# Gathered rows in eleven buffers, and a wait on TensorE in every third batch of gathers

## The chip, the cores and the metric

One core of a Trainium2 chip runs the kernel. The time is the device time of one launch in microseconds, the median of several runs on the same chip.

## The reference

One layer of a graph network on 12,500 nodes with 160 values each (64 scalars and 32 vectors of three) and 400,000 edges, which are sorted by their target node:

```python
h = jnp.maximum(_layernorm(x, axis=-1), 0.0)
x0 = h[:, :64]; x1 = h[:, 64:].reshape(n, 32, 3)
y0 = x0 @ W_l1_0 * a / 8                       # a: one value per node
y1 = einsum('nuc,uv->nvc', x1, W_l1_1) * a / sqrt(32)
w  = silu(edge_attr_16 @ fc_W1 / 4) @ fc_W2 / 8   # 192 weights per edge: w_a, w_b, w_c, w_d
ys0 = y0[src]; ys1 = y1[src]                   # a row of y for each edge
e0 = edge_attr_4[:, :1]; e1 = edge_attr_4[:, 1:]
mid_a = w_a * ys0 * e0
mid_d = w_d * einsum('euc,ec->eu', ys1, e1) / sqrt(3)
mid_b = (w_b * ys0)[:, :, None] * e1[:, None, :]
mid_c = (w_c * e0)[:, :, None] * ys1
z0 = zeros.at[dst].add(concat(mid_a, mid_d)); z1 = zeros.at[dst].add(concat(mid_b, mid_c))
out = x + self-connection of h + z0, z1 mapped by W_l2_0, W_l2_1
```

## The kernel before

**Stages.** First the nodes: layer norm, relu and the two maps, 8 tiles of 128 nodes at a time. The rows of y go to a table `y_d` in HBM, the self-connection into `acc`, which stays in SBUF. Then the edges in 3125 tiles of 128. Four tiles (`GT`) are a batch, 782 batches in all, and three batches (`K = TG // GT`) share one selection matrix of 12 tiles. Sums over edges of one target are matmuls with that selection matrix, gathered in PSUM over groups of 24 tiles (the first three fifths of the edges) or 12.

**One step of the edge loop.** Iteration `b` of the loop in the last part of the function does, in program order:

- `load_xe`: asks on SP's queue for the block of edge features that batch `b + AHEAD` needs.
- `weigh(b + 2)` (L609, L611): four matmuls on TensorE give the edge weights of a batch in PSUM (`pw`, two of them in turn), and then ACT puts three edge values of each edge beside them.
- `lift_rows(b + 2)` (L520): ACT multiplies the gathered rows by an edge value, into `yge`.
- `dots_of(b + 1)` (L525, L527) and `products(b + 1)` (L531, L532, L535, L536) on DVE; each third batch also `select` (L628).
- `load(b + AHEAD)` (L571 to L584, the gathers in L579): four indirect DMAs issued by POOL, each of 128 rows of `y_d` by the source numbers in `src_sb`, into one of `YB` buffers `yg`. A buffer is free again when DVE's L531 and ACT's L520 of its batch have read it.
- `sums(b)` (L648) on TensorE, and what belongs to a finished group (`turn`, `map_sums`, `accumulate`); each second batch `hidden` (L592, L597), the first layer of the edge network.

**Queues.** TensorE, ACT and DVE run in exactly this order, since the loop stands in a manual schedule. POOL and SP do not: their instructions are ordered by the tile framework, which puts a gather on POOL's queue when the things it waits for come, by its own reckoning. A POOL instruction that waits holds up all behind it.

**The wait by hand.** `load` gives the first gather of a batch (`k == 0`) one more thing to wait for: the last weight matmul of batch `b - AHEAD + 2`, whose name `weigh` has kept in `weighed`. With `YB = 9` and `AHEAD = YB + 1 = 10` that is eight batches back. The buffer itself came from the batch nine back.

**Made batches.** For 24 batches (48, 72, ... 432 and 498, 540, ... 750; all multiples of three) y is not gathered. The rows of x for them were gathered while the nodes were worked on (L375, into `xr`, a pool `nrx` of 12 buffers, then to `xr_d` in HBM), and TensorE, DVE and ACT make y from them in the gaps of the edge loop (`made_load` to `made_leave`). For such a batch `load` returns before the gathers and the wait.

**Ahead of the loop** nine batches are loaded (`min(YB, NB)`), then `load(YB)` for the tenth.

Of the kernel before, what the change touches and what calls it, by code (L numbers as in the profile page):

```python
# [29 lines left out]
SP = 256 - WN // 4  # L30
TG = 12
EG = 8
YB = 9
WIDE = 3, 5
GN = 8
HN = 2
# [9 lines left out]
def kernel(  # L46
# [31 lines left out]
    NB = (T + GT - 1) // GT  # L78
# [32 lines left out]
    def made(b):  # L111

        return made_at.index(b) if b in made_at else None
# [30 lines left out]

    ygp = ctx.enter_context(tc.tile_pool(name="yg", bufs=YB))

# [50 lines left out]
    def relate_edges(q, evp, lim):  # L197

        lo, hi = q * EG * TG, min((q + 1) * EG * TG, T)
        over = evp.tile([P, EG * TG], F32, name="over")  # L200
        up = evp.tile([P, EG * TG], F32, name="up")
        for g, k, t, n in runs_of(lo, hi):
            v = drel[:, t:t + k * n].rearrange("p (s t) -> p s t", t=n)
            o = over[:, t - lo:t - lo + k * n].rearrange("p (s t) -> p s t", t=n)
            nc.vector.tensor_tensor(o, v, lim[:, g:g + k].unsqueeze(2).to_broadcast([P, k, n]), ALU.is_ge)
            nc.vector.tensor_tensor(v, v, nbase[:, g:g + k].unsqueeze(2).to_broadcast([P, k, n]), ALU.add)
        nc.vector.tensor_reduce(fars[:, q:q + 1], over[:, :hi - lo], AX.X, ALU.max)

        nc.vector.tensor_scalar(up[:, :hi - lo], drel[:, lo:hi], float(WN), -float(WN), ALU.is_ge, ALU.mult)
        nc.vector.tensor_add(drel[:, lo:hi], drel[:, lo:hi], up[:, :hi - lo])  # L210

        nc.vector.scalar_tensor_tensor(drel[:, lo:hi], over[:, :hi - lo], float(2 * ZR), drel[:, lo:hi],
                                       op0=ALU.mult, op1=ALU.add)

    def any_far(cnt):

        nc.vector.tensor_reduce(far, fars, AX.X, ALU.max)
        nc.tensor.matmul(cnt, far, one, start=True, stop=True)
        nc.vector.tensor_scalar(far_i, cnt, 1.0, None, ALU.min)
# [67 lines left out]
    def load_xe(blk):  # L287

        if blk not in blocks:
            xe = ld.tile([P, 512], F32, name="xe")  # L290
            v = e16[blk * P:(blk + 1) * P, :].rearrange("(s k f) (h c) -> k s (f h) c", s=4, k=2, h=2)
            for k in range(2):
                nc.sync.dma_start(xe[:, 256 * k:256 * (k + 1)], v[k])
            blocks[blk] = xe

    def e4_load(q):

        if q * EG < NU and q not in raws:
            lo, hi = q * EG * TG, min((q + 1) * EG * TG, TP)
            raw = ld.tile([P, EG * TG, 4], F32, name="raw")  # L300
            nc.sync.dma_start(raw[:, :hi - lo, :].rearrange("p t c -> p (t c)"), e4[:, lo * 4:hi * 4])
            raws[q] = raw
# [26 lines left out]
    engines = {mybir.EngineType.PE, mybir.EngineType.Activation, mybir.EngineType.DVE}  # L329
    with (  # L330
        tc.tile_pool(name="nr", bufs=1) as nrp,
        tc.tile_pool(name="nrx", bufs=12) as nrx,
        tc.tile_pool(name="ny", bufs=2) as ny,
        tc.tile_pool(name="ns", bufs=3) as ns,
        tc.tile_pool(name="nh", bufs=4) as nh,
# [204 lines left out]
    with (  # L540
# [9 lines left out]
        leaving, weighed = [], {}  # L550
# [5 lines left out]
        def next_px():  # L556
            turns["px"] += 1
            return pxs[turns["px"] % 2]

        K = TG // GT  # L560
        AHEAD = YB + 1

        short = NB - 2 if NB > 1 and (NB - 1) * GT % TG else NB

# [3 lines left out]
        def tiles_of(b):  # L568
            return list(range(first_of(b), first_of(b + 1)))

        def load(b):  # L571
            r = made(b)
            if r is not None:
                rows[b] = xms[r]
                return
            yg = ygp.tile([P, GT, D], F32, name="yg")
            rows[b] = yg
            for k, t in enumerate(tiles_of(b)):
                ins = nc.gpsimd.indirect_dma_start(  # L579
                    out=yg[:, k, :], out_offset=None, in_=y_d,  # L580
                    in_offset=bass.IndirectOffsetOnAxis(ap=src_sb[:, t:t + 1], axis=0))
                if k == 0 and b - AHEAD + 2 in weighed:
                    tc.add_manual_dep(ins.ins, weighed[b - AHEAD + 2], mybir.DependencyInfo(
                        mybir.DependencyClass.Sync, mybir.DependencyReason.DATA), reason="no further ahead of the weights")  # L584

        def hidden(s):

            if 2 * s < NB:
                xe = blocks[s * 2 * GT // BT]
                r = slice(32 * (s % 4), 32 * (s % 4 + 1))  # L590
                ph = next_px()
                nc.tensor.matmul(ph, w1[r, :], xe[r, :], start=True, stop=True)  # L592
                leaving.append(lambda: activate(s, ph))
# [20 lines left out]
        def lift_rows(b):  # L614
            lifted[b] = part.tile([P, GT, D], F32, name="yge")
            lift(lifted[b], rows[b], e4_of(b), len(tiles_of(b)))
# [15 lines left out]
        def dots_of(b):  # L632
            tmp = part.tile([P, GT, 3, M1], F32, name="tmp")
            dot(tmp, wts[b], rows[b], len(tiles_of(b)))

        def products(b):
            pr = prod.tile([P, GT, PC], F32, name="pr")
            multiply(pr, wts.pop(b), rows.pop(b), lifted.pop(b), len(tiles_of(b)))
            prs[b] = pr
# [150 lines left out]
        def all_leave():  # L790
            todo = leaving[:]
            leaving.clear()
            for f in todo:
                f()

        order = tc.manual_schedule(engines={mybir.EngineType.PE, mybir.EngineType.Activation, mybir.EngineType.DVE})
        with order:
            e4_load(0)
            for blk in range(min(AHEAD - 1, NB - 1) * GT // BT + 1):
                load_xe(blk)  # L800
            for b in range(min(YB, NB)):
                load(b)
            relate_edges(0, part, lim)
            for s in range(3):
                hidden(s)
                all_leave()
            if NQ == 1:
                any_far(next_px()[0:1, 0:1])
            for pw in pws:
                nc.vector.tensor_copy(pw[:, :, SP:], iota[:, 0:WN].rearrange("p (k c) -> p k c", k=GT))  # L810
            for b in range(min(2, NB)):
                weigh(b)
                lift_rows(b)
            dots_of(0)
            if YB < NB:
                load(YB)
            select(0, wts[0])
            products(0)
            last_batch = [(t - 1) // GT for t in ends]
            turns_at, maps_at, adds_at = {}, {}, {}  # L820
            for g, e in enumerate(last_batch):
                at_end = e + 4 >= NB
                t = e + (1 if at_end else 2)
                m = t + (1 if at_end else 2 if (t + 2) % 2 else 3)
                turns_at.setdefault(t, []).append(g)
                maps_at.setdefault(m, []).append(g)
                a = m + (1 if at_end else 2)
                adds_at.setdefault(a + 1 if a == NB - 3 else a, []).append(g)
            for b in range(NB + 3):
                u, k = divmod(b, K)  # L830
                due(at_start, b)
                if b + AHEAD < NB:
                    load_xe((b + AHEAD) * GT // BT)
                if b < NB:
                    q, r = divmod(b, EG * K)
                    if r == 0:
                        e4_load(q + 1)
                    if r == EG * K - 8 and q + 1 < NQ:
                        relate_edges(q + 1, part, lim)
                    if r == EG * K - 4 and q + 2 == NQ:  # L840
                        any_far(next_px()[0:1, 0:1])
                if b + 2 < NB:
                    weigh(b + 2)
                all_leave()
                due(on_scalar, b)
                if b + 2 < NB:
                    lift_rows(b + 2)
                if b + 1 < NB:
                    dots_of(b + 1)
                    if k == K - 1:  # L850
                        select(u + 1, wts[b + 1])
                    products(b + 1)
                if b + AHEAD < NB:
                    load(b + AHEAD)
                for g in adds_at.get(b, []):
                    accumulate(g)
                    leave_before(g + 1)
                due(on_vector, b)
                if b < NB:
                    sums(b)  # L860
                for g in turns_at.get(b, []):
                    turn(g)
                for g in maps_at.get(b, []):
                    map_sums(g)
                if b % 2 == 0:
                    hidden((b + 6) // 2)
                due(on_tensor, b)
# [137 lines left out]
```

## Time and profile before

| | |
|---|---|
| median of 3 runs | 4818.65 us (4807.77 to 4824.67) |
| profiled execution | 4859.38 us, span 4857.6 us |
| mean granted TensorE clock | 0.905 |
| PE busy | 4063.7 us, 84% of the span |
| DVE busy | 3514.5 us, 72% |
| POOL busy | 2970.2 us, 61%, of which 2873.3 in 3029 gathers of L579 |
| ACT busy | 1762.0 us, 36% |
| DMA engines | 22.0% of 16 engines' span for the gathers' queue, 68 GB/s of HBM over the span |

Busy is the time in which an instruction of the engine runs. Behind the `<-` of a group stands what ended the idle time ahead of it: an engine with its tile and line, or `issue` where nothing that the profile shows was waited for. In the timeline a row gives the start, the duration, the engine and its line, and in brackets the idle time ahead of it.

### The profile page before, as it was taken

To read this page: it belongs to the slowest core of one execution; us is meant where nothing else is said; L and a number is where in the kernel's file an instruction comes from. 1 tells how busy PE (TensorE), PEld (TensorE's weight loads), DVE (VectorE), ACT (ScalarE), POOL (GpSimd) and SP (SyncE) were. 2 spreads that over 40 slices of the span, in tenths; PEclk is the share of its full clock that TensorE was granted. 3 is DMA by queue.
4 is the path that set the end of the run, shared out by engine and by line. 5 is a ranking of instruction groups with operands and counts; after the bars stand their busy time and mean duration, and the time that the engine had idled before them with its cause. 6 is when DMAs were issued, how large, how long until landed. Compare 5 with 4: busy or idle time off the path is not lost. (4 is left out here: it accounts for less than half of the span.)

```text
span 4857.6 us, 55990 instructions
## 1 busy us (share of the span) xinstructions
PE 4063.7 (84%) x16409; PEld 2349.2 (48%) x16409; DVE 3514.5 (72%) x6817; ACT 1762.0 (36%) x5610; POOL 2970.2 (61%) x3132
## 2 busy tenths in 40 slices
PE   5588888888888888888888888888888888888888
PEld 4344444444444444444444444454545455545554
DVE  4477777777777777777777776777777777777777
ACT  4333333333333333333333333333333333333333
POOL 6566566566666666666666666666666666666663
PEclk8788898999998889999999999899989999999899
DMA  7422222222222222222222222222222222232222
GB/s 212 122 60 60 63 65 62 64 61 62 63 66 64 62 65 61 62 63 66 65 62 66 62 64 61 63 63 64 66 58 66 61 65 61 65 104 61 62 61 59
DMA packets 228623, 335.20 MB, mean 69 GB/s; under 512 B 55099, under 2 KB 171911, under 8 KB 228055
## 3 DMA queue, kind: packets, MB, share of 16 engines
q0 software_dynamic: 150000, 256.20, 22.0%
q1 hardware_dynamic: 64642, 67.02, 4.5%
q10 hardware_dynamic: 13668, 8.36, 0.6%
q8 instruction: 130, 2.13, 0.2%
q14 instruction: 183, 1.49, 0.1%
HBM read 307.49 MB, written 23.88 MB: 68 GB/s over the span
## 5 line engine op out<-in xcount | busy, mean ns | idle before, releaser
L579 POOL DMA_INDIRECT yg<-y_d,src_sb x3029 | 2873.3, 949 | 1775.7 <-issue 827.8
L648 PE MATMUL pz<-pr,sel 128*128 128x384 f32 x6250 | 2515.7, 549 | 88.5 <-issue 59.9
L648 PEld LDWEIGHTS pz<-pr,sel 128*128 128x128 f32 x6250 | 1256.4, 211 | 1061.9 <-issue 508.9
L609 PE MATMUL pw<-w,hT 64*128 64x192 f32 x6250 | 833.3, 370 | 582.2 <-DVE pr L536 315.5
L611 ACT ACTIVATE pw<-raw 128x12 f32<-128x12 f32 (+1 forms) x782 | 140.2, 179 | 2973.4 <-remote 1215.2
L520 ACT ACTIVATE yge<-yg,raw 128x160 f32<-128x160 f32 x3029 | 1041.7, 421 | 0.0
L609 PEld LDWEIGHTS pw<-w,hT 64*128 64x128 f32 x6250 | 553.4, 197 | 974.9 <-issue 523.0
L525 DVE TENSOR_TENSOR tmp<-yg,pw 128x384 f32<-128x384 f32 (+1 forms) x758 | 416.0, 549 | 710.0 <-ACT pw L611 661.6
L532 DVE TENSOR_TENSOR pr<-pr,pw 128x768 f32<-128x768 f32 (+1 forms) x782 | 745.3, 953 | 27.0
L527 DVE TENSOR_REDUCE yg<-tmp 128x128 f32<-128x384 f32 (+1 forms) x758 | 450.0, 594 | 430.5 <-ACT yge L520 370.9
L628 DVE TENSOR_TENSOR sel<-pw,drel 128x1536 f32<-128x1536 f32 (+1 forms) x261 | 455.1, 1744 | 0.0
L592 PE MATMUL px<-xe,w 32*128 32x512 f32 x782 | 443.3, 649 | 13.5 <-issue 8.3
L531 DVE TENSOR_TENSOR pr<-pw,yg 128x384 f32<-128x384 f32 (+1 forms) x758 | 419.8, 554 | 17.8
L536 DVE TENSOR_TENSOR pr<-pw,yge 128x384 f32<-128x384 f32 (+1 forms) x782 | 427.9, 547 | 0.0
L535 DVE TENSOR_TENSOR pr<-pw,yge 128x256 f32<-128x256 f32 (+1 forms) x782 | 326.2, 417 | 0.0
L597 ACT ACTIVATE hT<-px 128x512 f32<-128x512 f32 x391 | 228.5, 585 | 11.3 <-PE px L592 10.5
L592 PEld LDWEIGHTS px<-xe,w 32*128 32x128 f32 x782 | 115.5, 185 | 214.1 <-issue 151.9
L675 PEld LDWEIGHTS px<-wc,za 128*128 128x128 f32 x1110 | 153.1, 196 | 40.4 <-issue 7.6
L693 DVE SCALAR_TENSOR_TENSOR acc<-os,by,acc 128x160 f32 x370 | 142.9, 386 | 14.8 <-ACT os L680 1.0
L675 PE MATMUL px<-wc,za 128*128 128x96 f32 x1110 | 151.8, 274 | 1.9 <-issue 1.3
L375 POOL DMA_INDIRECT xr<-in_x,src_sb x88 | 88.3, 1003 | 57.1 <-ACT hT L437 21.6
L662 PEld LDWEIGHTS pz<-ident,zs 128*128 128x128 f32 x555 | 72.5, 141 | 58.4 <-issue 34.4
(126 smaller groups left out, 1683.0 us busy)
## 6 DMA issues: line engine op xcount, KB each, us to landing
yg<-y_d,src_sb POOLq DMA_INDIRECT x3029
xe<-in_e SPq DMA_DIRECT2D x196, 128.0 KB
xr_d<-xr SPq DMA_DIRECT2D x24, 320.5 KB
y_d<-ys ACTq DMA_DIRECT2D x12, 640.0 KB
xm<-xr_d SPq DMA_DIRECT2D x24, 320.0 KB
acc<-in_x SPq DMA_DIRECT2D x11, 640.0 KB
out<-acc SPq DMA_DIRECT2D x11, 640.0 KB
raw<-in_e SPq DMA_DIRECT2D x32, 192.0 KB
```

The costliest lines, as they stand in the source:

```text
L520: nc.scalar.activation(yge[:, k, :], yg[:, k, :], AF.Copy, scale=e4v[:, k, 0:1])
L525: nc.vector.tensor_tensor(tmp[:, :n], y1, wt[:, :n, NW:NW + 3].unsqueeze(3).to_broadcast([P, n, 3, M1]), ALU.mult)
L527: nc.vector.tensor_reduce(yg[:, :n, M0:96], tmp[:, :n].rearrange("p t c u -> p t u c"), AX.X, ALU.add)
L531: nc.vector.tensor_mul(pr[:, :n, 0:96], wt[:, :n, 96:NW], yg[:, :n, 0:96])
L532: nc.vector.tensor_mul(pr[:, :n, 256:].rearrange("p t (c u) -> p t c u", c=3), pr[:, :n, 0:M0].unsqueeze(2).to_broadcast([P, n, 3, M0]), w ...
L535: nc.vector.tensor_mul(pr[:, :n, 96:160], wt[:, :n, 0:M0], yge[:, :n, 0:M0])
L536: nc.vector.tensor_mul(pr[:, :n, 160:256].rearrange("p t (c u) -> p t c u", c=3), wt[:, :n, M0:96].unsqueeze(2).to_broadcast([P, n, 3, M1] ...
L579: ins = nc.gpsimd.indirect_dma_start(out=yg[:, k, :], out_offset=None, in_=y_d, in_offset=bass.IndirectOffsetOnAxis(ap=src_sb[:, t:t + 1], ...
L592: nc.tensor.matmul(ph, w1[r, :], xe[r, :], start=True, stop=True)
L609: last = nc.tensor.matmul(pw[:, k, 0:NW], hids[s][r, o:o + P], w2[r, :], start=True, stop=True)
L628: nc.vector.tensor_tensor(sels[u][:, 0:n, :].rearrange("p t (k c) -> p t k c", k=GT), for_each, drel[:, u * TG:u * TG + n].unsqueeze(2).un ...
L648: nc.tensor.matmul(z_ps[g], sels[t // TG][:, t % TG, :], pr[:, k, M0:], start=first, stop=last)
```

## The change

The buffers `yg` grow from 9 to 11. `AHEAD`, which was tied to them, becomes 8 of its own: `load(b + 8)` stands in iteration `b`. The wait by hand stays on the first gather of a batch only where the batch's number is a multiple of three, and by the new `AHEAD` it is on the weights six batches back. Seven batches are loaded ahead of the loop and an eighth after the first dots. Blocks of edge features are asked for by the same `AHEAD`, two batches later. The `nrx` pool of the node stage goes from 12 buffers to 10.

```diff
-YB = 9
+YB = 11
+AHEAD = 8
...
-        tc.tile_pool(name="nrx", bufs=12) as nrx,
+        tc.tile_pool(name="nrx", bufs=10) as nrx,
...
         K = TG // GT
-        AHEAD = YB + 1
...
                 ins = nc.gpsimd.indirect_dma_start(
                     out=yg[:, k, :], out_offset=None, in_=y_d,
                     in_offset=bass.IndirectOffsetOnAxis(ap=src_sb[:, t:t + 1], axis=0))
-                if k == 0 and b - AHEAD + 2 in weighed:
+                if k == 0 and b % K == 0 and b - AHEAD + 2 in weighed:
                     tc.add_manual_dep(ins.ins, weighed[b - AHEAD + 2], mybir.DependencyInfo(
                         mybir.DependencyClass.Sync, mybir.DependencyReason.DATA), reason="no further ahead of the weights")
...
-            for b in range(min(YB, NB)):
+            for b in range(min(AHEAD - 1, NB)):
                 load(b)
...
-            if YB < NB:
-                load(YB)
+            if AHEAD - 1 < NB:
+                load(AHEAD - 1)
```

## The prediction

> **What bounds the kernel now.** I read the page first, then the busy time by stretches, the waits of DVE and ACT, and the timeline of POOL, PE, ACT and DVE over a hundred microseconds in the middle.
>
> ```profile
> span 4857.6 us, 55990 instructions
> PE 4063.7 (84%) x16409; PEld 2349.2 (48%) x16409; DVE 3514.5 (72%) x6817; ACT 1762.0 (36%) x5610; POOL 2970.2 (61%) x3132
> ...
> L579 POOL DMA_INDIRECT yg<-y_d,src_sb x3029 | 2873.3, 949 | 1775.7 <-issue 827.8
> ```
> ```profile
> 184.00:4806.00 4622.00, 3921.89 (x15647) 2235.57 (x15646) 3380.24 (x6361) 1653.68 (x5339) 2872.24 (x3029) 0.91 0.26 64
> ```
> ```profile
> DVE tmp L525 <- ACT pw L611: 673.9, 235, 16.8
> ```
>
> No engine is full. In the stretch in which POOL gathers (184 to 4806 us; columns: length, then PE, PEld, DVE, ACT, POOL, clock, DMA share, GB/s) PE is busy 3922 us of 4622. There are 3029 gathers of y and 24 made batches, which stand for 96 more, so 3125/4 = 781.25 batches in 4622 us: 5.92 us a batch. The wait that counts is DVE's for ACT's copy of the edge values (L611), 673.9 us: DVE cannot start the dot of a batch before ACT has seen that TensorE finished the weights (L609) and has run L611. The timeline shows why ACT is late. Here is one round of three batches.
>
> ```profile
> 2123.60 0.94 POOL L579 DMA_INDIRECT yg<-y_d,src_sb  x1 [3.15 <-ACT pw L611]
> ...
> 2137.34 0.94 POOL L579 DMA_INDIRECT yg<-y_d,src_sb  x1 [0.30 <-issue]
> 2141.47 0.94 POOL L579 DMA_INDIRECT yg<-y_d,src_sb  x1 [3.18 <-ACT pw L611]
> ```
> ```profile
> 2127.97 0.92 PE L609 MATMUL pw<-w,hT 64*128 64x192 f32 x8 [2.27 <-DVE pr L536]
> ...
> 2134.26 0.92 PE L609 MATMUL pw<-w,hT 64*128 64x192 f32 x8
> ...
> 2138.94 1.41 PE L609 MATMUL pw<-w,hT 64*128 64x192 f32 x8
> ```
> ```profile
> 2128.98 0.18 ACT L611 ACTIVATE pw<-raw 128x12 f32<-128x12 f32 x1 [1.96 <-DVE tmp L525]
> ...
> 2140.80 0.18 ACT L611 ACTIVATE pw<-raw 128x12 f32<-128x12 f32 x1 [9.86 <-PE pw L609]
> ```
> ```profile
> 2135.98 0.55 DVE L536 TENSOR_TENSOR pr<-pw,yge 128x384 f32<-128x384 f32 x1
> 2141.02 0.56 DVE L525 TENSOR_TENSOR tmp<-yg,pw 128x384 f32<-128x384 f32 x1 [4.50 <-ACT pw L611]
> ```
>
> The weights that start at 2127.97 end at 2128.89, and ACT goes on at 2128.98, 0.09 us later. The next weights end at 2135.18, and ACT, idle all that time, goes on only at 2140.80, 5.62 us later. TensorE's notice came early when POOL had five gathers behind it, and late when it had ten; it came 2.52 us after POOL's last gather had ended (2137.34 + 0.94 = 2138.28). So while POOL issues gathers back to back, the notices of TensorE are held, and they are let go some 2.5 us after POOL falls idle. DVE stood still for 4.50 us meanwhile. The round takes 2141.47 - 2123.60 = 17.87 us for three batches, 5.96 a batch: 11 steps of (2137.34 - 2123.60)/11 = 1.249 us, the twelfth gather and the idle time.
>
> Where POOL pauses in each batch, things go faster:
>
> ```profile
> 2159.68 0.94 POOL L579 DMA_INDIRECT yg<-y_d,src_sb  x1 [3.52 <-ACT pw L611]
> ...
> 2177.33 0.94 POOL L579 DMA_INDIRECT yg<-y_d,src_sb  x1 [0.30 <-issue]
> 2181.57 0.94 POOL L579 DMA_INDIRECT yg<-y_d,src_sb  x1 [3.29 <-remote]
> 2185.29 0.95 POOL L579 DMA_INDIRECT yg<-y_d,src_sb  x1 [2.78 <-issue]
> ...
> 2190.91 0.94 POOL L579 DMA_INDIRECT yg<-y_d,src_sb  x1 [0.92 <-ACT yge L520]
> ...
> 2196.45 0.94 POOL L579 DMA_INDIRECT yg<-y_d,src_sb  x1 [0.84 <-ACT yge L520]
> ```
>
> From 2185.29 to 2196.45 POOL issues 8 gathers in two runs of four with 0.92 and 0.84 us between, and a batch takes 11.16/2 = 5.58 us. Before it stands the round around a made batch, where POOL issues 15 gathers in one run (2159.68 to 2177.33): 2181.57 - 2159.68 = 21.89 us, 4.02 more than the ordinary round. So the price of a long run is that its hold lasts to its end, and it is POOL's waits that end runs.
>
> **The change part by part.** *Waits taken away.* Two of three batches lose their wait on TensorE. Where POOL is stopped by a held notice today, that is what lets the notice go; tomorrow POOL runs on to the next waiting gather or to a buffer that isn't free. What it saves on POOL itself is small: its semaphore waits there are
>
> ```profile
> L579 POOLq EVENT_SEMAPHORE  x1501: 17/42/7984, 181.2 to 4803.1; - x188
> ...
>   DVE tmp L525: 2.1, 1
> ```
>
> 1501 with a median of 42 ns; dropping a third saves 500 x 0.042 = 21 us at most, beside the 1.249 us steps, so between 0 and -21; I take 0. The second row says that one reader of gathered rows waited for the gather, 2.1 us in all, so the data are early by far today.
>
> *The wait that stays, six batches back.* POOL's queue isn't written out by hand, so a gather goes on it as soon as its buffer is free. The waiting gather needs weights that come later than its buffer does (eleven back), so I expect it behind gathers of the next batches, about nine ahead of the weights it waits for, much as far as today. Either way POOL has one wait on TensorE for 12 gathers. If it falls as in the round above, the round stays at 12 gathers: 12 x 1.249 + (3.18 - 0.30) = 17.87 us. So an ordinary round is today's longest regular one, always.
>
> *Made batches.* The made batches are 48, 72, ... 432 and 498, 540, ... 750, all multiples of three, so `load` returns for them before the wait: those 24 rounds have no wait at all. POOL goes from 12 to 12 + 8 = 20 gathers in one run: 20 x 1.249 + 2.88 = 27.86 us, in which no more than the three batches of an ordinary round get through, since the notices are held from about the sixth gather on. Against today's 21.89 that is +5.97 us, 24 times: +143. After it POOL is ahead and is stopped by buffers again; if that buys three more batches at 5.58 instead of 5.96, it gives back 3 x 0.38 x 24 = -27. Sum +116. Bounds: 0, if a free-buffer wait cuts the run, to +143 with nothing given back.
>
> *Ordinary rounds.* By 5.96 a batch for all, with three batches at 5.58 behind each long run, today's loop would be 24 x (21.89 + 3 x 5.58) + (781.25 - 144) x 5.957 = 927 + 3796 = 4723 us. It took 4622, so 101 us come from other stretches in which POOL is stopped in each batch. Two thirds of those stops are gone, so I count two thirds of it lost: +67, between 0 and +101.
>
> *Eleven buffers.* No arithmetic changes. In before no round waits for a landing (2.1 us above), and gathers still have six batches of 5.9 us, 35 us, less a run of 15 to 25; cost 0, and one batch of 5.9 us wherever that cover fails.
>
> *Setup.* Ten buffers for xr instead of twelve, and seven batches loaded ahead of the loop, not nine.
>
> ```profile
> POOL yg L579 <- DMA xr_d<-xr: 25.9, 1, 25.9
> POOL xr L375 <- issue: 21.9, 72, 0.3
> ```
>
> POOL waits 25.9 us before the first gather of y, and 72 of the 96 gathers of x wait for nothing but the 0.3 us step. Two buffers fewer can delay them, but the wait of 25.9 us covers it: 0, at most +10 (two batches of four steps) without that cover. Blocks of edge features are asked for two batches later; SP waits for their buffers anyway:
>
> ```profile
> SPq L293 <- remote: 745.4, 18, 62.6
> ```
>
> So 0, and +1 us a block where it would be late.
>
> *Sum.* +116 + 67 = +183 us on the profiled execution, 4859.38 us (span 4857.6) to 5042, 3.8%. The median of the runs shown is 4818.65, 0.8% under the profiled one; with the same 183 us it becomes 5000.
>
> A rule weighed. The row: data are waited for 2.1 us in the whole kernel. The Trainium skill, page "DMA: Bandwidth & Descriptors", section "Rules for kernel authors", says to issue a DMA early, compute, and wait late, so that its fixed cost is covered; by it a looser wait does no harm, and the change would be worth about 0. Its "~2.0 us" of fixed cost and 436 GB/s would make an estimate of 2.2 us for a gather of 82 KB, which the lead covers. That is the first rival, and 183 us is what row and rule differ by.
>
> **The rivals.** *Nothing changes.* The round of 12 is already common and its period is set by POOL, not by who waits. All ordinary rounds at 17.87 us, and the made ones at three batches of 5.58 = 16.74: 236.4 x 17.87 + 24 x 16.74 = 4626 us against 4622, a median of about 4822. For it: the steadiness of the round. Against it: the long runs at made batches, which nothing in the change cuts.
>
> *Faster.* With eleven buffers and few waits on TensorE POOL gets so far ahead that a free buffer stops it in each batch, as at 2190.91 and 2196.45; the pauses of 0.8 to 0.9 us then keep the notices early. All batches at 5.58 give 781.25 x 5.58 = 4359 us, -263, a median of 4556; half of them, 4687. For it: those rows. Against it: POOL falls out of that state in before within 20 us, and then has a wait per batch to help it back.
>
> *Much slower.* The waiting gather stands one batch worse, so that a buffer wait splits the round: one gather, then a pause till the row product of the first batch (DVE's L531) is done, 3.18 us after ACT's L611, then eleven gathers.
>
> ```profile
> 2122.94 0.18 ACT L611 ACTIVATE pw<-raw 128x12 f32<-128x12 f32 x1 [9.60 <-remote]
> ```
> ```profile
> 2125.56 0.56 DVE L531 TENSOR_TENSOR pr<-pw,yg 128x384 f32<-128x384 f32 x1
> ```
>
> (2125.56 + 0.56 - 2122.94 = 3.18.) The pause replaces a step of 1.249 by some 3.2, so a round costs +2 us, 260 times: +520, a median near 5340. It decides when that pause comes in most rounds and doesn't shorten the hold behind it.
>
> **How the numbers follow.** Forecast (a loss of some 1 to 8%) 0.56; nothing changes 0.15 (0.05 on each side and within); faster 0.17; much slower 0.12. That makes 0.22 faster by over 0.3%, about what a measurement of this kernel can tell, 0.05 within, 0.73 slower. The range of the forecast goes from +60 to +400 (long runs at half price, to all of the bounds and a third of the split rounds); it is widened to 4740 below, for the second case and the mild part of the third, and ends at 5220. Outside stay most of the faster case and the worst of the slow one.
>
> **What would show it.** Right: POOL's timeline has runs of 12 and some of about 20 gathers, fewer idle spells than now, each of 3 us; ACT's L611 follows L609 at once in a run's first half and only 2.5 us after POOL's last gather in the second; DVE's wait for L611 grows from 673.9 to 800 us or more; a made round takes about 28 us. Wrong: runs cut to four with pauses under 1 us (faster); notices early in long runs (then POOL isn't what holds them); or L525 waiting for gathers, which would mean that the lead is too short.

## The result and the profile after

The changed kernel takes 5124.76 us (median of 4, 5116.04 to 5127.76) against 4816.74 us before (4 runs): 1.0637 times the time before, 95% interval 1.0614 to 1.066. The profiled execution took 5127.76 us, 268 us more than that of before. Lines 34 to 560 of before have a number one higher now: DVE's L525, L531 and L536 are L526, L532 and L537, ACT's L520 is L521; L579, L609, L611 and L648 kept their numbers. A notice is the signal by which one engine tells another that it is done; a set of weights is what four matmuls of L609 leave for one batch.

The page, busy times and clock first, then the costliest groups:

```profile
span 5126.0 us, 55478 instructions
PE 4138.0 (81%) x16409; PEld 2374.9 (46%) x16409; DVE 3513.1 (69%) x6817; ACT 1763.0 (34%) x5610; POOL 2962.7 (58%) x3132
...
L579 POOL DMA_INDIRECT yg<-y_d,src_sb x3029 | 2866.4, 946 | 2043.7 <-PE pw L609 886.9
```

DVE, ACT and POOL are busy for as long as before, to 8 us. What grew is idle time: POOL's before its gathers from 1775.7 to 2043.7 us, of which the profile now puts 886.9 down to TensorE's weights. PE's busy time grew by 74 us with the same number of instructions: its clock was granted at 0.87 instead of 0.91 in the stretch of the gathers, which is now 4885 us long instead of 4622:

```profile
193.40:5078.40 4885.00, 4003.26 (x15668) 2263.81 (x15668) 3384.23 (x6371) 1656.62 (x5346) 2866.40 (x3029) 0.87 0.24 61
```

DVE's wait for ACT's copy, which was 673.9 us, and a wait of TensorE that the prediction did not have (it was 59.9 us before):

```profile
DVE tmp L526 <- ACT pw L611: 894.9, 226, 12.9
...
PE pz L648 <- issue: 177.9, 158, 2.3
```

POOL's timeline says where the time went: an ordinary round, then one with a made batch.

```profile
2134.21 0.94 POOL L579 DMA_INDIRECT yg<-y_d,src_sb  x1 [4.39 <-issue]
...
2151.51 0.94 POOL L579 DMA_INDIRECT yg<-y_d,src_sb  x1 [2.61 <-remote]
...
2175.26 0.95 POOL L579 DMA_INDIRECT yg<-y_d,src_sb  x1 [0.30 <-issue]
2199.77 0.94 POOL L579 DMA_INDIRECT yg<-y_d,src_sb  x1 [23.56 <-DVE pr L532]
```

The ordinary round has 12 gathers and takes 2151.51 - 2134.21 = 17.30 us. The next has 20, (2175.26 - 2151.51)/1.25 + 1, and then POOL stands for 23.56 us: 48.26 us until it goes on, and six batches are computed in it. Counting all runs of gathers (a run ends where POOL idles over 0.6 us): 203 runs of 12 with a mean of 17.59 us, and 23 of 20 with a mean of 48.03, 3570 and 1105 of the 4885 us. Runs of 1 to 8, of which before had 221, are down to six of 2. What happens in the long round:

```profile
2163.55 0.92 PE L609 MATMUL pw<-w,hT 64*128 64x192 f32 x8
...
2167.82 0.92 PE L609 MATMUL pw<-w,hT 64*128 64x192 f32 x8
2168.68 1.56 PE L648 MATMUL pz<-pr,sel 128*128 128x384 f32 x4
2172.00 0.48 PE L648 MATMUL pz<-pr,sel 128*128 128x384 f32 x1 [1.77 <-issue]
2174.12 0.48 PE L648 MATMUL pz<-pr,sel 128*128 128x384 f32 x1 [1.64 <-issue]
...
2187.82 1.65 PE L609 MATMUL pw<-w,hT 64*128 64x192 f32 x8 [2.21 <-DVE pr L537]
```
```profile
2158.19 0.18 ACT L611 ACTIVATE pw<-raw 128x12 f32<-128x12 f32 x1 [2.95 <-PE pw L609]
...
2179.80 0.18 ACT L611 ACTIVATE pw<-raw 128x12 f32<-128x12 f32 x1 [19.48 <-remote]
```

The weights of 2163.55 end at 2164.47 and ACT goes on with them at 2179.80, 15.33 us later and 3.59 after POOL's last gather ended (2176.21). In the meantime TensorE's own matmuls come singly, some 2 us apart, with nothing waited for that the profile shows. Then ACT, DVE and TensorE start again one after the other, and the next weights run 20.00 us after the last ones (2187.82 - 2167.82), where those two stand 4.27 apart. After that batches follow each other at 4.6 to 6.1 us by the same timeline, while POOL stands and waits for the weights six batches back; the profile names L532, which only happened to end last.

### The profile page after: what moved, and what is told of

Same layout as the page of the kernel before. It is cut to its first block, busy times and chain, and to the rows that moved or that the text cites. A ratio compares the mean times of both kernels' runs of the same rounds, so it can differ in the third digit from the quotient of the medians.

```text
span 5126.0 us, 55478 instructions
## 1 busy us (share of the span) xinstructions
PE 4138.0 (81%) x16409; PEld 2374.9 (46%) x16409; DVE 3513.1 (69%) x6817; ACT 1763.0 (34%) x5610; POOL 2962.7 (58%) x3132
## 4 chain that ended last, share of the span: by engine, by line
PE 44%; another core or an unknown queue 18%; ACT 13%; DVE 12%; issue 10%; POOL 1%; ACTq 1%; DMA 1%; DVEq 0%; SPq 0%; POOLq 0%
PE pz L648 25%; PE pw L609 13%; ACT yge L521 7%; PE px L592 4%; DVE yg L528 3%; DVE pr L532 3%; DVE pr L537 2%; DVE pr L536 2%; POOL yg L579 1%; DVE pr L533 1%; PE px L675 1%; ACTq L611 1%; DVE sel L628 1%; ACT hT L597 1%
## 5 line engine op out<-in xcount | busy, mean ns | idle before, releaser
L579 POOL DMA_INDIRECT yg<-y_d,src_sb x3029 | 2866.4, 946 | 2043.7 <-PE pw L609 886.9
L648 PE MATMUL pz<-pr,sel 128*128 128x384 f32 x6250 | 2592.3, 560 | 179.5 <-issue 177.9
L648 PEld LDWEIGHTS pz<-pr,sel 128*128 128x128 f32 x6250 | 1282.4, 216 | 1192.9 <-issue 720.4
L609 PE MATMUL pw<-w,hT 64*128 64x192 f32 x6250 | 814.5, 382 | 575.9 <-DVE pr L537 452.8
L611 ACT ACTIVATE pw<-raw 128x12 f32<-128x12 f32 (+1 forms) x782 | 140.1, 179 | 3229.4 <-PE pw L609 1699.4
L526 DVE TENSOR_TENSOR tmp<-yg,pw 128x384 f32<-128x384 f32 (+1 forms) x758 | 416.0, 549 | 955.3 <-ACT pw L611 894.5
L521 ACT ACTIVATE yge<-yg,raw 128x160 f32<-128x160 f32 x3029 | 1041.7, 421 | 0.3 <-issue 0.3
L609 PEld LDWEIGHTS pw<-w,hT 64*128 64x128 f32 x6250 | 552.3, 205 | 961.1 <-DVE pr L537 608.9
L592 PE MATMUL px<-xe,w 32*128 32x512 f32 x782 | 460.7, 672 | 96.4 <-ACT hT L597 88.6
L532 DVE TENSOR_TENSOR pr<-pw,yg 128x384 f32<-128x384 f32 (+1 forms) x758 | 420.0, 554 | 17.8
L537 DVE TENSOR_TENSOR pr<-pw,yge 128x384 f32<-128x384 f32 (+1 forms) x782 | 428.3, 548 | 0.0
L536 DVE TENSOR_TENSOR pr<-pw,yge 128x256 f32<-128x256 f32 (+1 forms) x782 | 326.4, 417 | 0.0
```

Of the source, the lines that this page charges most:

```text
L521: nc.scalar.activation(yge[:, k, :], yg[:, k, :], AF.Copy, scale=e4v[:, k, 0:1])
L526: nc.vector.tensor_tensor(tmp[:, :n], y1, wt[:, :n, NW:NW + 3].unsqueeze(3).to_broadcast([P, n, 3, M1]), ALU.mult)
L532: nc.vector.tensor_mul(pr[:, :n, 0:96], wt[:, :n, 96:NW], yg[:, :n, 0:96])
L536: nc.vector.tensor_mul(pr[:, :n, 96:160], wt[:, :n, 0:M0], yge[:, :n, 0:M0])
L537: nc.vector.tensor_mul(pr[:, :n, 160:256].rearrange("p t (c u) -> p t c u", c=3), wt[:, :n, M0:96].unsqueeze(2).to_broadcast([P, n, 3, M1] ...
L579: ins = nc.gpsimd.indirect_dma_start(out=yg[:, k, :], out_offset=None, in_=y_d, in_offset=bass.IndirectOffsetOnAxis(ap=src_sb[:, t:t + 1], ...
```

## The experiments

The first four kernels ran on one chip, where the kernel before took 4854.22 us (7 runs), the next four on another, where it took 4811.59 us (7 runs). Each ratio is against the kernel before on the same chip.

**A wait behind made batches.** The changed kernel with

```diff
-                if k == 0 and b % K == 0 and b - AHEAD + 2 in weighed:
+                if k == 0 and (b % K == 0 or made(b - 1) is not None) and b - AHEAD + 2 in weighed:
```

> The changed kernel with one wait more: behind a made batch the first gathered batch of the triple waits too, for the weights six batches back. Theory A (the loss lies in the 24 made rounds, where POOL issues 20 gathers without a wait and TensorE's notices are held to the end): the run of 20 falls into 12 and 8, its six batches take some 34 us instead of 48, so 24 x 14 = 336 us less than the changed kernel: 4790 us, between 4740 and 4850. Rival B (the loss comes from the wait being six batches back on TensorE, in all rounds): only 24 waits of 260 are added, so 5050 to 5130.

4919.11 us, ratio 1.0119 (1.0086 to 1.0153): a miss by 70 us, but far from rival B. POOL's timeline around a made batch (the starts of a run of 12, of the run of 8 behind it, and of the run after that):

```profile
2046.89 0.94 POOL L579 DMA_INDIRECT yg<-y_d,src_sb  x1 [2.85 <-remote]
...
2074.08 0.94 POOL L579 DMA_INDIRECT yg<-y_d,src_sb  x1 [12.49 <-PE pw L609]
...
2085.86 0.94 POOL L579 DMA_INDIRECT yg<-y_d,src_sb  x1 [2.08 <-PE pw L609]
```

There is no run of 20 left. The run of 12 ahead of the new wait takes 27.19 us and the run of 8 behind it 11.78, on average over the 24 places 25.68 + 12.24 = 37.9 us for six batches, against 48.0. That is 24 x 10.1 = 243 us, close to the step from 1.0119 to 1.0637 (5.2%, 250 us; the two were measured on different chips). Why the run of 12 took 27 us and not 17.6 is not shown. My reading is that the wait behind it is for a fourth set of weights: three fall into a run of 12, the last of them let go when POOL stops, and for a fourth ACT, DVE and TensorE have to get going first. The kernel that was to test this (seven back, below) ran where no notice is held.

**A wait on every batch again.** The changed kernel without `b % K == 0`.

> The changed kernel with the wait on every gathered batch again, six batches back. Theory A: no run can be longer than the batches whose weights are let go together, so runs of 12, 8 and 4 as in the kernel before; 4650 to 4830 us, no run of 20. Rival B (six back is the loss): 5050 or more, since every batch then waits for late weights.

4767.41 us, ratio 0.9822 (0.9803 to 0.9841). It is faster than before, with eleven buffers and six back. There are 122 runs of 12, 144 of 8 and 77 of 4, and only one of 13 or more. Rival B is out: the distance isn't the loss. Between this kernel and the one with waits behind made batches, on the same chip, lie 3.0%: that is the price of the waits that the latter lacks. It isn't paid in the ordinary rounds. Timed by the starts of ACT's L611, of which each batch has one, the four rounds that end with a made batch's own take 1758 us in sum over the 24 places, against 1577 here; the other 164 rounds take 2933 and 2951 us, 17.9 and 18.0 each. So far from a made batch the missing waits cost nothing, and all of the price falls around the made ones.

**Only every third wait, in the kernel before.**

```diff
-                if k == 0 and b - AHEAD + 2 in weighed:
+                if k == 0 and b % K == 0 and b - AHEAD + 2 in weighed:
```

> The kernel before (nine buffers, weights eight back) with the wait on every third batch only. Theory A: the made rounds have no wait on TensorE here either, but with nine buffers POOL is stopped by a buffer that is not free in the middle of the 20 gathers, so the runs stay at 12 or below: 4600 to 4850 us. Rival C (taking away two of three waits is the loss by itself, whatever the buffers): 5050 to 5130.

5070.83 us, ratio 1.0445 (1.0401 to 1.049). Theory A's range is missed and rival C's just reached: with nine buffers the loss is there as well. There are 22 runs of 16 gathers, 26.94 us each with a pause of 7.2, and 40 runs of a single gather with a pause of 4.1 us in the middle one (before has 40 too, of 2.8). A buffer that isn't free does stop POOL, but it stops it later than the wait would have, or after one gather.

**A wait on DVE instead of TensorE.** The changed kernel, each batch waiting for the last product (L537) of seven batches back.

```diff
+            done[b] = multiply(...).ins.name    # multiply returns its last product, L537
...
-                if k == 0 and b % K == 0 and b - AHEAD + 2 in weighed:
-                    tc.add_manual_dep(ins.ins, weighed[b - AHEAD + 2], ...
+                if k == 0 and b - AHEAD + 1 in done:
+                    tc.add_manual_dep(ins.ins, done[b - AHEAD + 1], ...
```

> The changed kernel, but every gathered batch waits for DVE's last product seven batches back instead of TensorE's weights. Theory A (only TensorE's notices are held while POOL issues; DVE's are not): POOL stops in each batch within four to eight gathers, the notices stay prompt, a batch takes 5.0 to 5.6 us: 781.25 x 5.3 + 240 = 4380 us, between 4150 and 4640. Rival D (POOL's issue isn't what holds the notices): runs and time as in the kernel before, 4780 or more.

5646.61 us, ratio 1.1643 (1.1601 to 1.1685), the slowest of all and the worst miss. It lies in rival D's range, but not with the runs of the kernel before, as D had it; the loads by SP below decide against D. 116 runs have 16 gathers, 28.69 us each. POOL, TensorE, ACT and DVE at the end of 16 gathers (a pause of 0.68 us in them makes them runs of 6 and 10 in the count):

```profile
2130.80 0.95 POOL L579 DMA_INDIRECT yg<-y_d,src_sb  x1 [0.30 <-issue]
2139.86 0.95 POOL L579 DMA_INDIRECT yg<-y_d,src_sb  x1 [8.11 <-DVE m_own L758]
```
```profile
2123.30 0.92 PE L609 MATMUL pw<-w,hT 64*128 64x192 f32 x8
```
```profile
2134.45 0.18 ACT L611 ACTIVATE pw<-raw 128x12 f32<-128x12 f32 x1 [12.78 <-issue]
```
```profile
2139.04 0.55 DVE L537 TENSOR_TENSOR pr<-pw,yge 128x384 f32<-128x384 f32 x1
```

The weights that end at 2124.22 reach ACT at 2134.45, 10.23 us late and 2.70 after POOL's last gather (2131.75). But POOL doesn't wait for them: it waits for a product of DVE, which comes 5.14 us later still (2139.59). That suggests that the wait that stops POOL should be for the very thing that is let go when it stops. Long runs came all the same: in this one three more products of DVE end while POOL issues, the last at 2126.22, so that the next waits are met on the way.

**Loads by SP in place of the gathers,** all of them, or the second and fourth of each batch:

```diff
-                ins = nc.gpsimd.indirect_dma_start(...)
+                c = t * P % (N - P)
+                ins = nc.sync.dma_start(yg[:, k, :], y_d[c:c + P, :])
```

> The changed kernel with the gathers left out: SP's queue loads 128 consecutive rows of y for each tile instead, of the same bytes, into the same buffers and with the same waits. (The rows are not those of the edges.) Theory A (POOL's issuing holds TensorE's notices): no notice is held, L611 follows the weights within 0.1 to 0.2 us, and a batch takes the 4.6 to 5.0 us that it takes while POOL stands still: 781.25 x 4.8 + 240 = 3990 us, between 3800 and 4200. Rival D (the notices are late for another cause, such as the traffic or TensorE's own queue): 4700 us or more, with waits of L611 of 5 us and more as before.

> The changed kernel with every other gather (the second and fourth tile of a batch) loaded by SP instead, as consecutive rows; those rows are not the edges'. Theory A (notices are held from about the sixth gather of a run on): an ordinary round has 6 gathers in 7.5 us and the made rounds 10, so hardly a hold is left in the ordinary rounds and some in the made ones: 3900 to 4300 us. Rival E (one gather in flight is enough to hold notices, or a mixture of queues does it): 4500 or more.

3797.29 us (3 us below theory A's range) and 3971.55 us (inside it) in one run each, beside 4811.59 for the kernel before on that chip. Both kernels keep the changed kernel's waits. TensorE and ACT without gathers (here L609 and L611 are L608 and L610):

```profile
2100.45 0.92 PE L608 MATMUL pw<-w,hT 64*128 64x192 f32 x8
```
```profile
2101.46 0.18 ACT L610 ACTIVATE pw<-raw 128x12 f32<-128x12 f32 x1 [1.99 <-PE pw L608]
```

0.09 us after the end (2101.37), and in no such place over 0.38: where ACT stood idle when weights ended, it went on over 1 us late 0 times in 757 without gathers and 60 times in 735 with half of them, against 309 in 506 in the profile of before, and 316 in 527 in the kernel with more buffers alone (below) on the same chip. The bytes are the same; what is gone is POOL's gathers. With half of them an ordinary round has 6 and takes 13.7 us for three batches. So on that chip the late notices come with POOL's back-to-back gathers, and as many bytes by SP's queue don't bring them. Whether it is POOL's issuing or the reading of scattered rows isn't separated, since SP loaded consecutive ones.

**Buffers alone, distance alone.** The kernel before with `YB = 11`, `AHEAD = 10` and ten buffers for x; and the kernel with a wait on every batch, six back, with `YB = 9`.

> The kernel before with eleven buffers (and ten for x), and all else as it was: each batch waits for the weights eight back. The step from the kernel before to the changed one with the wait on every batch gave 0.982. Theory F (what helps is that no gather waits for a buffer, that is for DVE's products, any more): 0.975 to 0.99 here too, and fewer runs of one gather with a pause. Rival G (the distance of six batches is what helps): 0.995 to 1.01 here.

> The changed kernel with the wait on every batch, six back, and nine buffers instead of eleven. Theory F: with the wait six back a buffer nine back is long free, so nothing waits for buffers here either: 0.975 to 0.99. Rival G: 0.975 to 0.99 as well. If neither buffers nor distance alone do it, 0.99 to 1.01 in both.

0.9792 (0.9776 to 0.9808) and 0.9796 (0.978 to 0.9813): each alone gives what both give (0.9822, on another chip). The kernel before has 40 runs of a single gather, like the one at 621.17 here:

```profile
621.17 0.94 POOL L579 DMA_INDIRECT yg<-y_d,src_sb  x1 [1.54 <-remote]
624.89 0.94 POOL L579 DMA_INDIRECT yg<-y_d,src_sb  x1 [2.78 <-issue]
```
```profile
623.59 0.56 DVE L531 TENSOR_TENSOR pr<-pw,yg 128x384 f32<-128x384 f32 x1
```

The pause ends 0.74 us after L531 has set a buffer free (623.59 + 0.56 = 624.15). Neither of the two kernels has a single such run: with two more buffers, or with loads two batches later, the buffer is free in time. The longest semaphore wait of POOL ahead of a gather was 7.98 us before and is 0.04 us in both. Rival G falls, and theory F fits: 40 pauses of 2.7 us on average, where a step has 0.3, are 97 us, and the gain is 100.

**Shorter leads, and a chip where nothing is held.** Three more kernels: the wait behind made batches for the weights seven back; a wait on every batch four back (`AHEAD = 6`); and three back.

> The changed kernel with a wait behind made batches as in e1_made_wait, but for the weights seven back, so that the run of 12 ahead of it waits for three more weights and not four; the run of 8 behind it waits for three, not two. Theory H (three weights fit into a run of 12, the third comes with the notices let go when POOL stops; a fourth needs TensorE, ACT and DVE started again and costs some 10 us more: 27.3 us where 17.6 is usual): the run of 12 falls from 25.7 us on average to 17.7, the run of 8 rises from 12.2 to 16 to 22; in sum -4 to +2 us a made round, ratio to before 0.99 to 1.02. Rival I (the extra time at made batches belongs to the made batch's own work): the run of 12 stays at 25 or more and the run of 8 rises, ratio 1.03 to 1.06.

> The changed kernel with the wait on every batch and four back instead of six (loads stand six ahead in the program). If the long runs live on POOL being several batches behind what it may gather, a shorter lead leaves less room for that: runs of 12 give way to 8 and 4, ratio to before 0.94 to 0.98. If the runs are set by how many notices are let go at once (three), whatever the lead, the ratio is 0.975 to 0.99 as with six back. If data come late, over 1.0, and DVE or ACT wait for the gathers.

> The same with three back (loads stand five ahead; the blocks of edge features are asked for eight ahead as in the changed kernel). By the first reading 0.92 to 0.98, by the second 0.975 to 0.99; a lead of three batches less a run of 8 or 12 is short, so over 1.0 if rows come late.

The kernel before took 3956.57 us (25 runs) on the chip on which these ran, and all three 1.0024 times that (1.0014 to 1.0034). The second of them ran once more, on another chip:

> The kernel of f4_four_back once more, for a chip on which notices are held. Where the kernel before takes 4800 us or more: 0.94 to 0.975 if a lead of four batches breaks up the runs of 12, 0.975 to 0.99 if the lead doesn't matter (six and eight back gave 0.98), over 1.0 if rows come late. Where the kernel before takes some 3957 us, no notice is held and POOL's steps of 1.249 us are the bound: 1.00 again.

3959.68 us before (13 runs), 1.0024 again (1.0014 to 1.0033). POOL and, from two timelines of the kernel with four back on the first of these chips, TensorE and ACT:

```profile
L579 POOL DMA_INDIRECT yg<-y_d,src_sb x3029: 942/946/1104, 151.7 to 3941.7; - x190
```
```profile
2117.04 0.92 PE L609 MATMUL pw<-w,hT 64*128 64x192 f32 x8
```
```profile
2118.05 0.18 ACT L611 ACTIVATE pw<-raw 128x12 f32<-128x12 f32 x1 [0.94 <-ACT yge L521]
```

3029 gathers from 151.7 to 3941.7 us are (3941.7 - 151.7)/3028 = 1.252 us each: POOL never stops, and the notice comes 0.09 us after the weights, 0 times in 679 over 1 us late. On these two chips the bound is POOL's step, no wait that was tried matters, and the readings for which the three kernels were made stay open. The changed kernel itself was not run there.

## Why the prediction was right, point by point

The forecast (slower, by long runs of gathers that hold TensorE's notices) came true; 5125 us lies in the range, 125 us above the predicted 5000. The size was short by a third, 183 us against 268 between the profiled executions, and one part of it stood in the wrong place, as the points below say.

- **Held notices.** The reading of one round of before carried it, and the loads by SP bear it out. The traces do too: of the sets of weights that found ACT idle, those that ended with nine or more gathers of a run issued were over 1 us late every time (121 of 121 before, 193 of 193 after), those with up to four 34 times in 113 before and 0 in 44 after. But a hold need not last to the end of a run: of 300 late sets that ended within a run of before, ACT went on with 52 while the run still went.
- **Ordinary rounds of 12.** Predicted 17.87 us, measured 17.59 on 203 of them: -57 us in sum.
- **Made rounds.** The run of 20 is there, 23 times. Predicted 27.86 + 3 x 5.58 = 44.6 us for six batches, measured 48.03: +82 us. The sign "a made round takes about 28 us" didn't come: the 20 gathers take 25 us, and POOL then stands for 23. What failed is the thought that three batches go through as in any round: ACT got one set of weights at once (2158.19), two were held to the end, and TensorE itself stalled.
- **The give-back of -27** was counted twice, since the round of today that I compared with had those three quick batches already.
- **Stops lost elsewhere.** I took two thirds of 101 us, +67. All of them went: in the trace after hardly a run shorter than 12 is left, so +34. But they didn't lie elsewhere. Timed by L611 as above, the four rounds that end with a made batch's own take 1663 us before and 1986 after, +323; the other 164 rounds take 2970 and 2904, -66. The quick stretches of before stood around the made batches, and away from them the change costs nothing.
- **Setup.** I took 0 and bounded it at +10. The first gather stands at 193.4 us instead of 183.8: +9.6. It fits the chips without held notices, where three kernels that share the ten x buffers and the later loads were all 9 us slower. The ten buffers cost it: with them and the loads as before ("buffers alone") the first gather stands at 193.7 us, and with twelve ("only every third wait, in the kernel before") at 182.8. With ten the gathers of x end 8 to 10 us later, and the wait of 25.9 us behind them covers nothing of that.

```profile
L579 POOL DMA_INDIRECT yg<-y_d,src_sb x3029: 940/946/1109, 183.8 to 4805.9; - x190
```
```profile
L579 POOL DMA_INDIRECT yg<-y_d,src_sb x3029: 940/946/1104, 193.4 to 5077.5; - x190
```

Those rows are of before and of after. In sum 183 - 57 + 82 + 27 + 34 + 10 = 279, against 268 between the two profiled executions. The medians are 308 us apart, since the profiled execution of before was 43 us above its median and that of after 3.

- **Eleven buffers at 0** was wrong in another way. By the runs the change is a sum of three: -1.8% from buffers and distance, +3.0% from taking away the waits that the kernel with waits behind made batches lacks (paid around the made batches, as shown above), +5.2% from the wait behind each made batch (the last step compares two chips). The first was hidden by the others. The pause behind a single gather that I priced in the rival "much slower" was there in before, and the two buffers took it away.
- **The rivals.** "Nothing changes" and "faster" fell on this chip. "Much slower" didn't come: with eleven buffers there is no run of a single gather. With nine there are 40, in before as in the kernel at 1.0445, and not the 260 that the rival needs.

The rule of the Trainium skill that I weighed (page "DMA: Bandwidth & Descriptors", section "Rules for kernel authors": issue early, wait late) made the change worth about 0. The two chips without held notices agree with it: there no placing of the waits that was tried moves more than the setup's 9 us. Where the kernel before takes 4.8 ms the measurement decides against it: waiting less costs 6%.

## What to carry to other kernels

On some chips gathers issued without pause delayed the notices of an engine that had no part in them, so look at how long after an engine's end its reader goes on, and what a third engine did meanwhile. A wait that looks useless for the data may be what lets the notices through; when it is made rarer, check the places where it falls out altogether, here the made batches: the whole loss lay in the rounds around them. And try to wait for the thing that comes when you stop: behind a run of 12 POOL paused some 3 us for TensorE's weights, and behind one of 16 almost 9 us for DVE's products.

## What the runs showed of the hardware

The holding differs from chip to chip: on the chips of three measurements the kernel before took 4812 to 4854 us, on two others 3957 and 3960, with the same instructions. What sets them apart wasn't found. In a hold of 15 us TensorE's own matmuls stall too, at some 2 us apart. And a stalled TensorE comes back slowly: in the round of 48.26 us the granted clock was 0.75 on average, against 0.90 in the round ahead of it, and the weights at 2187.82 took 1.65 us instead of 0.92.

```profile
2134.21:2151.51 17.30, 15.34 (x56) 8.07 (x55) 12.79 (x24) 4.36 (x17) 11.35 (x12) 0.90 0.24 57
2151.51:2199.77 48.26, 31.76 (x114) 17.35 (x114) 30.11 (x65) 17.10 (x51) 18.91 (x21) 0.75 0.16 40
```

The Trainium skill, page "TensorE: Matmul & The Clock Gate", section "What's actually happening", has the clock fall to half after an idle window of about 3.4 us; the two rows agree in kind.
